# The last epilogue of a four-layer selective-scan network, run as four streams

## The chip, the cores and the metric

The kernel runs on one core of one Trainium2 chip. The metric is the device time of one execution in microseconds (us); smaller is better. The kernel before takes 21146.67 us, the median of three runs (21117.39, 21146.67 and 21153.36 us). One further execution was recorded by the hardware profiler; all profile numbers below are from that one.

A core has five engines, each with an instruction queue of its own: TensorE (PE) multiplies matrices and writes its sums to PSUM banks, VectorE (DVE) does elementwise work and scans, ScalarE (ACT) evaluates functions such as Exp, Ln and Silu, GpSimd (POOL) does elementwise work here, and SyncE (SP) issues the transfers (DMAs). An instruction waits at the head of its queue until the semaphores that it needs have been raised.

## The reference

The input is eight images of 48 by 48 positions and 96 channels. Four layers follow each other, each of the form x + ss2d(gn(x)), where gn normalises groups of three channels. Cut to what matters here, ss2d of a layer is:

```python
xz = x @ in_proj                       # 96 -> 2 * 192 channels
xc, z = split(xz)
xc = silu(depthwise_conv3x3(xc) + conv_b)
# four sequences: rows, columns, and both reversed
for each sequence: dt, B, C = projections of xc; delta = softplus(dt ...)
    h[t] = h[t-1] * exp(delta * A) + delta * u * B ; y[t] = sum_n h[t] * C
y = sum of the four sequences + D * xc
y = (y - mean(y)) * rsqrt(var(y) + eps) * g + b     # over the 192 channels
y = y * silu(z)
return y @ out_proj                    # 192 -> 96 channels
```

In the last layer the scan is written with cumulative sums (decay = exp(cumsum(...)), h = decay * cumsum(dB_u / (decay + 1e-12))). The last three lines of the block, together with z = x @ in_proj and the sum with x, are what this document calls the epilogue.

## The kernel before, in words

Two images form a pair, so each of the four layers has four pairs, and sixteen pairs are worked through one after the other. The 192 channels of two images are laid out as three tiles of 128 partitions. A pair has three parts. The **prologue** (`prologue`) normalises x, projects it, does the 3 by 3 convolution as nine products per block of rows (L301), and projects the scans' inputs. The **scans** are the main work: units that each handle some of the 16 states of one sequence. In the last layer only the first and last 192 positions of each sequence are scanned (class `Edge`): a pair has 48 units, twelve groups of four. The **epilogue** (`epilogue`) takes the sum y of the scans back from DRAM in 16 chunks of three image rows (144 positions) and finishes the layer.

`run` writes the program. Its loop goes over all units of all pairs. For each unit it writes the unit's own instructions: on ACT the logarithm and inverse of the decays (L887, L888) and four exponentials (L880); on PE the spreading of B (L893) and, four units late, the sum over states (L913); on DVE two products (L898, L899) and four scans (L901); on POOL two products (L905, L906). Beside it, it takes steps from two generators: the prologue of the following pair and the epilogue of the pair before. In the last layer up to ten such steps are written per unit. They begin at the fifth unit of a pair, and what is left of them is written in one go (`drain`) when the pair's last group of four units is reached. `prepare`, the softplus for the next group, is written in the first two units of each group (L585 to L614); it holds one of the two PSUM banks of the pool `psum` from its product L585 to L614.

After the last pair's scans nothing else is left to do beside it, and its epilogue is written by `drain(epilogue(*pairs[-1]))`: 16 chunks, one after the other. One chunk is this chain (line numbers of the kernel before):

1. PE: y minus its mean, as products with a centring matrix (L956, L957, L961, L962), into a PSUM bank.
2. ACT: copy to `eyc` (L996) and square into `ey` (L997); also the normalised x, `exn` (L990).
3. PE: minus the mean of the squares (L956 to L962 again).
4. ACT: Ln and Exp, together the inverse root (L1006, L1007).
5. DVE: product (L1009). ACT: gain and shift (L1012). PE: z (L1018, L1022).
6. ACT: Silu (L259), with a table load before it and another (L260) after it. DVE: product (L1031).
7. PE: x plus the output projection, twelve products (L1057, L1058, L1059). ACT: copy to `eo` (L1063). SP: two stores (L1065).

The loads of a chunk (`ex`, L972, and `ey`, L974) are issued in the middle of the chunk before it; both tiles have two buffers.

The generated order is not always the order of execution. The framework's scheduler sorts the instructions of each engine by its own model of costs. `keep_order(a, b)` takes this freedom away for a stretch of the program: it ties each instruction of an engine to the one written before it. The stretch is given by marks, that is by positions in the program that `mark()` appends to the list `marks`:

```python
        mark()                                  # once, before the first unit
...
            if l in short and unit == 0:
                mark()
...
    keep_order(*marks[:2])
```

`short` holds the last layer alone. In the kernel before, the stretch from the first unit to the first mark of the last layer keeps its written order; the last layer is left to the scheduler. A second program for the last layer behind a condition (`tc.If`) is not executed with these inputs.

Of the kernel before, what the change touches and what calls it, by code (L numbers as in the profile page):

```python
# [39 lines left out]
F32 = mybir.dt.float32  # L40
# [9 lines left out]
P = 128  # L50
NB, H, W, DM = 8, 48, 48, 96
# [18 lines left out]
BANK = 512  # L70
# [5 lines left out]
ECHUNKS = [(r * W, min(EROWS, H - r) * W) for r in range(0, H, EROWS)]  # L76
# [26 lines left out]
def ss2d_layers_kernel(ctx: ExitStack, tc: tile.TileContext, x_in, consts, weights, out):  # L103
# [14 lines left out]
    tmp = ctx.enter_context(tc.tile_pool(name="tmp", bufs=3))  # L118
# [131 lines left out]
    state = {}  # L250
# [11 lines left out]
    def bank():  # L262
        return psum.tile([P, BANK], F32, name="ps", tag="ps")
# [388 lines left out]
    class Chunk:  # L652
# [47 lines left out]
        def load(self, n):  # L700

            s, m, at = state[self.l, self.p], self.m, slice(self.c0, self.c0 + self.m)
            if n == 0:
                self.brow = rpool.tile([2 * NR, SCAN], BF16, name="brow", tag="brow")
                for j, b in enumerate(self.batches):
                    nc.sync.dma_start(
                        self.brow[NR * j : NR * j + NR, :m],
                        s["xb"][self.ph, b, :, self.d, :, at],
                    )
            row = 2 * layers[self.l].rank + 2 * NS * self.d + NS + n  # L710
            self.cb[n] = cb = cbpool.tile([P, SCAN], F32, name="cb", tag="cb")
            for b in self.batches:
                o = cb[64 * b : 64 * b + 64] if self.t == 2 else cb
                rows = s["xd"][self.ph, b, row : row + 1, at]
                nc.sync.dma_start(
                    o[:, :m], rows.to_broadcast([64 if self.t == 2 else P, m])
                )
# [221 lines left out]
                nc.sync.dma_start(s["yd"][t], y)  # L939


    def epilogue(l, p):
        ly, s = layers[l], state[l, p]
        gn, yd, src = s["gn"], s["yd"], x_store(l, p)
        dst = x_store(l + 1, p) if l + 1 < NLAYER else None
        EM = EROWS * W

        def half(b):
            return slice(64 * b, 64 * b + 64)

        def over_channels(ps, z, own, own_2, tiles):


            for t in tiles:
                if t < 2:
                    nc.tensor.matmul(ps[:, t, :], own, z[:, t, :], start=True, stop=False)  # L956
                    nc.tensor.matmul(ps[:, t, :], off_2[:, t, :], z[:, 2, :], start=False, stop=True)  # L957
                    continue
                for b in range(2):
                    o = ps[half(b), 2, :]  # L960
                    nc.tensor.matmul(o, off[:, 0:64], z[:, b, :], start=True, stop=False)  # L961
                    nc.tensor.matmul(o, own_2[:, half(b)], z[:, 2, :], start=False, stop=True)  # L962

        def three():
            return bank()[:, : 3 * EM].rearrange("p (t m) -> p t m", t=3)

        loaded = {}

        def load(i):
            at = slice(ECHUNKS[i][0], sum(ECHUNKS[i]))  # L970
            x = sm2.tile([DM, 2, EM], F32, name="ex", tag="ex")
            nc.sync.dma_start(x, src[:, :, at].rearrange("b c m -> c b m"))  # L972
            y = sm2.tile([P, 3, EM], F32, name="ey", tag="ey")
            nc.sync.dma_start(y, yd[:, :, at].rearrange("t p m -> p t m"))  # L974
            loaded[i] = x, y

        load(0)
        for _ in range(3):
            yield
        for i, (c0, m) in enumerate(ECHUNKS):  # L980
            at = slice(c0, c0 + m)
            x, y = loaded.pop(i)

            ps = three()
            over_channels(ps, y, centre, centre_22, (0, 1))
            yield True
            over_channels(ps, y, centre, centre_22, (2,))
            xn = sm1.tile([DM, 2, EM], F32, name="exn", tag="exn")
            for b in range(2):
                nc.scalar.activation(  # L990
                    xn[:, b, :], x[:, b, :], AF.Identity,
                    bias=gn[:, b, 1:2], scale=gn[:, b, 0:1],
                )
            yield True
            yc = sm1.tile([P, 3, EM], F32, name="eyc", tag="eyc")
            nc.scalar.copy(yc, ps)  # L996
            nc.scalar.activation(y, ps, AF.Square)  # L997
            yield

            ps = three()  # L1000
            over_channels(ps, y, off, off_22, (0, 1))
            yield True
            over_channels(ps, y, off, off_22, (2,))
            yield True

            nc.scalar.activation(ps, ps, AF.Ln, bias=ln_eps, scale=-1.0)  # L1006
            nc.scalar.activation(ps, ps, AF.Exp, scale=-0.5)  # L1007
            yield True
            nc.vector.tensor_mul(yc, yc, ps)  # L1009
            yield  # L1010
            for t, ts in ((0, slice(0, 2)), (2, slice(2, 3))):
                nc.scalar.activation(  # L1012
                    yc[:, ts, :], yc[:, ts, :], AF.Identity,
                    bias=ly.column(t, C_B), scale=ly.column(t, C_G),
                )
            ps = three()
            for t in range(2):
                nc.tensor.matmul(  # L1018
                    ps[:, t, :], ly.inw[:, DIN : DIN + P], xn[:, t, :], start=True, stop=True
                )  # L1020
            for b in range(2):
                nc.tensor.matmul(  # L1022
                    ps[half(b), 2, :], ly.inw[:, DIN + P : 2 * DIN], xn[:, b, :],
                    start=True, stop=True,
                )
            if i + 1 < len(ECHUNKS):
                load(i + 1)
            yield True
            silu(ps, ps)
            yield True  # L1030
            nc.vector.tensor_mul(yc, yc, ps)  # L1031
            yield
            if dst is not None:
                ps = bank()[0:DM, : 2 * EM].rearrange("p (b m) -> p b m", b=2)
                for b in range(2):
                    nc.tensor.matmul(
                        ps[:, b, :], ident[0:DM, 0:DM], x[:, b, :], start=True, stop=False
                    )
                    nc.tensor.matmul(
                        ps[:, b, :], ly.outw[:, 0, :], yc[:, b, :], start=False, stop=False  # L1040
                    )
                    nc.tensor.matmul(
                        ps[:, b, :], ly.outw_2[:, b, :], yc[:, 2, :], start=False, stop=True
                    )
                yield True
                nc.scalar.copy(x, ps)
                yield
                nc.sync.dma_start(dst[:, :, at].rearrange("b c m -> c b m"), x)
                continue

            q = m // 2
            ps = bank()[:q, : 4 * DM].rearrange("q (h b c) -> q h b c", h=2, b=2)
            for h in range(2):
                z = slice(h * q, h * q + q)
                for b in range(2):
                    o = ps[:, h, b, :]
                    nc.tensor.matmul(o, x[:, b, z], ident[0:DM, 0:DM], start=True, stop=False)  # L1057
                    nc.tensor.matmul(o, yc[:, b, z], ly.outw[:, 0, :], start=False, stop=False)  # L1058
                    nc.tensor.matmul(o, yc[:, 2, z], ly.outw_2[:, b, :], start=False, stop=True)  # L1059
            yield True  # L1060
            st = sm2.tile([P, 4, DM], F32, name="eo", tag="ld")
            st = st[:q].rearrange("q (h b) c -> q h b c", h=2)
            nc.scalar.copy(st, ps)  # L1063
            for b in range(2):
                nc.sync.dma_start(  # L1065
                    out[2 * p + b, at, :].rearrange("(h q) c -> q h c", h=2), st[:, :, b, :]
                )
            yield
        del state[l, p]


    def drain(g):
        for _ in g:
            pass
# [22 lines left out]
    def mark():  # L1097
        marks.append(len(tc._region_blocks()[0].instructions))

    def keep_order(a, b):  # L1100

        last = {}
        info = mybir.DependencyInfo(mybir.DependencyClass.NoSync, mybir.DependencyReason.DATA)
        for i in tc._region_blocks()[0].instructions[a:b]:
            if i.engine in ENGINES:
                if i.engine in last:
                    tc.add_manual_dep(i, last[i.engine], info, reason="order")
                last[i.engine] = i.name
# [5 lines left out]
    def run(pairs, short):  # L1114
# [102 lines left out]
            c.add_up(n)  # L1217
            catch_up()
        collected()
        drain(epilogue(*pairs[-1]))  # L1220

    last = NLAYER - 1
    run([(l, p) for l in range(NLAYER) for p in range(NPAIR)], (last,))

    keep_order(*marks[:2])


    every = sm1.tile([P, 1], F32, name="every", tag="every")
# [102 lines left out]
```

## Time and profile before

| what | us |
|---|---|
| median of three runs | 21146.67 |
| the profiled execution | 21131.57 |
| its span, first to last instruction | 21129.7 |
| last layer, pair 0 (first L880 of the pair to that of the next) | 19223.6 to 19650.4 |
| pair 1 | 19650.4 to 20087.8 |
| pair 2 | 20087.8 to 20522.8 |
| pair 3, to its last sum (L935) | 20522.8 to 20893.0 |
| last epilogue, first product to end of the last copy | 20900.2 to 21122.9 |

| engine | busy us in the span | share |
|---|---|---|
| PE | 18566.6 | 88% |
| DVE | 18834.4 | 89% |
| ACT | 13520.6 | 64% |
| POOL | 17984.5 | 85% |

The profile is read by stretches here, because the shares of the whole span are those of the three long layers. In a line of the table of stretches, the numbers are the start and end, the length, then for PE, PEld (TensorE's loading of weights), DVE, ACT and POOL the busy time and, in brackets, the number of instructions; then the clock that was granted to TensorE as a share of the full one, the share of DMA time, and GB/s. In the chain, each line is a start, a duration, and the engine and line that the end of the program hung on at that moment.

### The profile page before, as it was taken

Reading aid. Unit: us, or ns where it says so; the run is one execution under the profiler, and the core shown is the slowest. Engines: PE = TensorE matmul, PEld = TensorE weight load, DVE = VectorE, ACT = ScalarE, POOL = GpSimd, SP = SyncE. Lnnn points to the kernel's source line nnn. Section 1 sums busy time; section 2 is a strip of 40 time slices with the busy share of each in tenths; the row PEclk is TensorE's granted clock in tenths of the full one; section 3 lists DMA queues with packets and bytes.
Section 4 is the critical chain, followed back from the end, with each engine's and each line's share of the span. In section 5 each row is a group of like instructions: output and inputs, shape, how many; then the busy total and the mean of one; then the engine's idle time right before and its main releaser. Section 6 shows DMA issues by size and latency. Waiting matters only on the chain. (4 is left out here: it accounts for less than half of the span.)

```text
span 21129.7 us, 229163 instructions
## 1 busy us (share of the span) xinstructions
PE 18566.6 (88%) x64610; PEld 9118.1 (43%) x64610; DVE 18834.4 (89%) x15938; ACT 13520.6 (64%) x23969; POOL 17984.5 (85%) x11081
## 2 busy tenths in 40 slices
PE   8988998998998998998998988998998998988886
PEld 3333444443444443443443443443443443444555
DVE  6999999999999999999999999999999999997453
ACT  5555666666666665665666666665665666667776
POOL 5999898898899899898899989898999899896442
PEclk8999999999999999999999999999999999999887
DMA  4666666676676676676676666666666666674221
GB/s 137 195 193 193 188 196 194 190 196 195 190 200 195 192 201 195 190 204 191 191 204 195 191 194 195 190 197 190 191 197 193 190 196 195 189 194 123 79 74 51
DMA packets 1707632, 3832.96 MB, mean 181 GB/s; under 512 B 238448, under 2 KB 575216, under 8 KB 1693168
## 3 DMA queue, kind: packets, MB, share of 16 engines
q1 hardware_dynamic: 1706352, 3818.21, 61.9%
q8 instruction: 521, 8.54, 0.2%
q14 instruction: 759, 6.22, 0.1%
HBM read 3665.08 MB, written 152.27 MB: 181 GB/s over the span
## 5 line engine op out<-in xcount | busy, mean ns | idle before, releaser
L804 PE MATMUL acc<-cb,cst 128*128 128x384 f32 x27648 | 10706.0, 516 | 0.0
L768 POOL TENSOR_TENSOR cb<-cb,da 128x768 f32<-128x768 f32 x5184 | 9349.5, 1813 | 1393.2 <-DVE da L759 875.6
L804 PEld LDWEIGHTS acc<-cb,cst 128*128 128x128 f32 x27648 | 5003.6, 196 | 3957.4 <-issue 1498.2
L759 DVE TENSOR_TENSOR_SCAN da<-da,carry,b 128x768 f32<-128x768 f32 x3456 | 6268.3, 1814 | 220.9 <-ACT b L726 3.7
L755 DVE TENSOR_TENSOR b<-du,b 128x768 f32<-128x768 f32 x5184 | 4912.0, 948 | 685.4 <-PE b L743 678.8
L726 ACT ACTIVATE da<-dl,a 128x768 f32<-128x768 f32 x5184 | 4770.4, 926 | 95.6 <-POOL cb L768 60.4
L743 PE MATMUL b<-brow,pick 48*128 48x512 bf16 (+3 forms) x10368 | 2652.0, 337 | 1581.8 <-DVE da L759 1239.4
L726 ACT ACTIVATE b<-dl,a 128x768 f32<-128x768 f32 x1728 | 1560.3, 903 | 2960.1 <-DVE da L759 2817.4
L698 POOL TENSOR_TENSOR bb<-bb,du 128x768 f32<-128x768 f32 x1728 | 3131.3, 1812 | 183.4 <-DMA bb<-xd 142.8
L768 POOL TENSOR_TENSOR cb<-cb,bb 128x768 f32<-128x768 f32 x1728 | 3134.0, 1814 | 161.5 <-issue 56.8
L759 DVE TENSOR_TENSOR_SCAN da<-da,b 128x768 f32<-128x768 f32 x1728 | 3030.5, 1754 | 110.2 <-ACT b L726 2.4
L743 PEld LDWEIGHTS <-pick 48*128 48x128 bf16 (+1 forms) x10368 | 669.2, 97 | 4379.9 <-DVE da L759 2363.1
L759 DVE TENSOR_TENSOR_SCAN bb<-b,carry,bb 128x768 f32<-128x768 f32 x1152 | 2069.3, 1796 | 5.9 <-ACT b L726 2.2
L301 PE MATMUL ps<-pad,diag 128*128 128x480 f32 (+1 forms) x4320 | 2015.0, 565 | 15.1 <-DVE du L611 9.6
L650 ACT COPY carry<-da 128x1 f32<-128x1 f32 x3456 | 627.1, 181 | 1086.3 <-DVE da L759 1076.4
L590 ACT ACTIVATE ps<-ps,w 128x384 f32<-128x384 f32 (+1 forms) x912 | 497.1, 545 | 1027.5 <-PE ps L585 1022.9
L301 PEld LDWEIGHTS ps<-pad,diag 128*128 128x128 f32 x4320 | 804.2, 193 | 725.2 <-issue 330.3
L603 POOL TENSOR_TENSOR lg<-lg,w 128x384 f32<-128x384 f32 (+1 forms) x912 | 892.4, 978 | 195.0 <-ACT w L601 194.8
L585 PE MATMUL ps<-dts,w 6*128 6x384 f32 (+5 forms) x2432 | 821.2, 523 | 240.6 <-DVE du L611 99.9
L759 DVE TENSOR_TENSOR_SCAN bb<-b,bb 128x768 f32<-128x768 f32 x576 | 1000.1, 1736 | 16.3 <-POOL bb L698 9.8
L604 POOL TENSOR_TENSOR lg<-lg,e 128x384 f32<-128x384 f32 (+1 forms) x912 | 889.5, 975 | 71.2
L798 PE MATMUL acc<-y,cst 128*128 128x384 f32 x1008 | 619.1, 745 | 192.2 <-ACT y L819 127.2
(141 smaller groups left out, 17243.9 us busy)
## 6 DMA issues: line engine op xcount, KB each, us to landing
cb<-xd SPq DMA_DIRECT2D x4736, 384.0 KB
cb<-xd SPq DMA_DIRECT2D x4736, 192.0 KB
bb<-xd SPq DMA_DIRECT2D x1152, 384.0 KB
bb<-xd SPq DMA_DIRECT2D x1152, 192.0 KB
yd<-y SPq DMA_DIRECT2D x48, 1152.0 KB
ey<-yd SPq DMA_DIRECT2D x256, 216.0 KB
brow<-xb SPq DMA_DIRECT2D x576, 72.0 KB
ex<-xs SPq DMA_DIRECT2D x256, 108.0 KB
```

The source lines that it names most:

```text
L301: nc.tensor.matmul(ps[:, :m], ly.diag[:, int(t == 2), j, :], pad[:, r0 + dy : r0 + dy + nr, dx : dx + W], start=(j == 0), stop=(j == 8),)
L585: nc.tensor.matmul(o[:, :m], ly.dtw[q0 : q0 + r, k, chans], dts[q0 : q0 + r, at], start=True, stop=True,)
L603: nc.gpsimd.tensor_sub(lg, lg, w1)
L604: nc.gpsimd.tensor_add(lg, lg, e)
L650: nc.scalar.copy(*late_act.pop(0))
L698: nc.gpsimd.tensor_mul(b, b, self.du)
L726: nc.scalar.activation(da, self.dl, AF.Exp, scale=columns_of(self.l, self.t, self.ph, self.d, n))
L743: nc.tensor.matmul(b[:, z : z + zm], w, self.brow[:k, z : z + zm], start=True, stop=True)
L755: nc.vector.tensor_mul(b, self.du, b)
L759: nc.vector.tensor_tensor_scan(way(h), way(da), way(b), start, ALU.mult, ALU.add)
L768: nc.gpsimd.tensor_mul(c, c, h)
L804: nc.tensor.matmul(self.acc[:, a, : self.m // 2], ident, c[:, a, :], start=False, stop=(n == NS - 1 and not self.turns),)
```

## The change

The epilogue of the last pair becomes four generators. Stream 0 takes chunks 0, 4, 8 and 12, stream 1 takes 1, 5, 9 and 13, and so on. `run` steps through them in turns; stream i is left out until turn 3 * i, so each begins three steps behind the one ahead of it. A chunk has twelve steps. Streams 0 and 1 take their PSUM tiles from `psum`, streams 2 and 3 from `pb`, the pool of the scans' B (two buffers each). Streams 1 to 3 hold x, the normalised x, y and its centred form in one tile `ew` of the pool `tmp` (three buffers, otherwise used by prologues) and load a chunk when they begin it; stream 0 loads ahead as before. Two marks are set around the streams, and a second `keep_order` is added.

```diff
+        def own_bank():
+            return bank() if part < 2 else pb.tile([P, 2 * BANK], F32, name="b", tag="b")
...
         def load(i):
             at = slice(ECHUNKS[i][0], sum(ECHUNKS[i]))
-            x = sm2.tile([DM, 2, EM], F32, name="ex", tag="ex")
+            if part:
+                w = tmp.tile([P, 10 * EM], F32, name="ew", tag="tmp")
...
+            else:
+                x = sm2.tile([DM, 2, EM], F32, name="ex", tag="ex")
+                y = sm2.tile([P, 3, EM], F32, name="ey", tag="ey")
+                xn = yc = None
...
-        load(0)
+        mine_of = range(part, len(ECHUNKS), parts)
+        load(part)
         for _ in range(3):
             yield
-        for i, (c0, m) in enumerate(ECHUNKS):
+        for i in mine_of:
+            c0, m = ECHUNKS[i]
             at = slice(c0, c0 + m)
-            x, y = loaded.pop(i)
+            if i not in loaded:
+                load(i)
+            x, y, xn, yc = loaded.pop(i)
...
-            if i + 1 < len(ECHUNKS):
-                load(i + 1)
+            if not part and i + parts < len(ECHUNKS):
+                load(i + parts)
...
-        drain(epilogue(*pairs[-1]))
+        mark()
+        streams = [epilogue(*pairs[-1], part, 4) for part in range(4)]
+        turn = 0
+        while streams:
+
+            streams = [g for i, g in enumerate(streams) if turn < 9 and turn < 3 * i or next(g, g) is not g]
+            turn += 1
+        mark()
...
     keep_order(*marks[:2])
+    keep_order(*marks[2:4])
```

The instructions of the epilogue and their shapes are the same; the lines of the changed kernel are numbered 1 to 22 higher from L957 on (L956 is L957, L996 is L1018, L1006 is L1028, L1012 is L1034, L1031 is L1053, L1057 is L1079, L1063 is L1085, L1065 is L1087).

More of the change, by code (lines that the diff above doesn't have):

```diff
@@ L939, in collect, with epilogue @@
                 nc.sync.dma_start(s["yd"][t], y)
-    def epilogue(l, p):
+    def epilogue(l, p, part=0, parts=1):
         ly, s = layers[l], state[l, p]
@@ L962, in over_channels @@
                     nc.tensor.matmul(o, own_2[:, half(b)], z[:, 2, :], start=False, stop=True)
+        def own_bank():
+            return bank() if part < 2 else pb.tile([P, 2 * BANK], F32, name="b", tag="b")
         def three():
-            return bank()[:, : 3 * EM].rearrange("p (t m) -> p t m", t=3)
+            return own_bank()[:, : 3 * EM].rearrange("p (t m) -> p t m", t=3)
         loaded = {}
@@ L970, in load @@
             at = slice(ECHUNKS[i][0], sum(ECHUNKS[i]))
-            x = sm2.tile([DM, 2, EM], F32, name="ex", tag="ex")
+            if part:
+                w = tmp.tile([P, 10 * EM], F32, name="ew", tag="tmp")
+                x, xn = (
+                    w[:DM, a * EM : a * EM + 2 * EM].rearrange("p (b m) -> p b m", b=2)
+                    for a in (0, 2)
+                )
+                y, yc = (
+                    w[:, a * EM : a * EM + 3 * EM].rearrange("p (t m) -> p t m", t=3)
+                    for a in (4, 7)
+                )
+            else:
+                x = sm2.tile([DM, 2, EM], F32, name="ex", tag="ex")
+                y = sm2.tile([P, 3, EM], F32, name="ey", tag="ey")
+                xn = yc = None
             nc.sync.dma_start(x, src[:, :, at].rearrange("b c m -> c b m"))
-            y = sm2.tile([P, 3, EM], F32, name="ey", tag="ey")
             nc.sync.dma_start(y, yd[:, :, at].rearrange("t p m -> p t m"))
-            loaded[i] = x, y
-        load(0)
+            loaded[i] = x, y, xn, yc
+        mine_of = range(part, len(ECHUNKS), parts)
+        load(part)
         for _ in range(3):
             yield
-        for i, (c0, m) in enumerate(ECHUNKS):
+        for i in mine_of:
+            c0, m = ECHUNKS[i]
             at = slice(c0, c0 + m)
-            x, y = loaded.pop(i)
+            if i not in loaded:
+                load(i)
+            x, y, xn, yc = loaded.pop(i)
             ps = three()
@@ L987, in epilogue @@
             over_channels(ps, y, centre, centre_22, (2,))
-            xn = sm1.tile([DM, 2, EM], F32, name="exn", tag="exn")
+            if xn is None:
+                xn = sm1.tile([DM, 2, EM], F32, name="exn", tag="exn")
             for b in range(2):
@@ L994, in epilogue @@
             yield True
-            yc = sm1.tile([P, 3, EM], F32, name="eyc", tag="eyc")
+            if yc is None:
+                yc = sm1.tile([P, 3, EM], F32, name="eyc", tag="eyc")
             nc.scalar.copy(yc, ps)
@@ L1051, in epilogue @@
             q = m // 2
-            ps = bank()[:q, : 4 * DM].rearrange("q (h b c) -> q h b c", h=2, b=2)
+            ps = own_bank()[:q, : 4 * DM].rearrange("q (h b c) -> q h b c", h=2, b=2)
             for h in range(2):
@@ L1068, in epilogue @@
             yield
-        del state[l, p]
+        state[l, p]["left"] = state[l, p].get("left", parts) - 1
+        if not state[l, p]["left"]:
+            del state[l, p]
     def drain(g):
```

## The prediction

> **What bounds the kernel now.** I read the page first, for the place of the stretch in the span.
>
> ```profile
> span 21129.7 us, 229163 instructions
> ...
> PE   8988998998998998998998988998998998988886
> ...
> POOL 5999898898899899898899989898999899896442
> PEclk8999999999999999999999999999999999999887
> ```
>
> Each digit is 528 us. Only the last is about the stretch that the change names: TensorE at 0.6, POOL at 0.2, and a granted clock of 0.7. So the next view is the table of stretches: the last layer's pairs 0 to 3, then what follows its last sum.
>
> ```profile
> 19223.00:19650.00 427.00, 355.95 (x1804) 239.15 (x1803) 228.80 (x403) 340.94 (x635) 194.07 (x136) 0.91 0.31 87
> 19650.00:20088.00 438.00, 368.87 (x1982) 255.25 (x1982) 225.11 (x394) 344.33 (x643) 191.98 (x135) 0.88 0.27 75
> 20088.00:20522.00 434.00, 366.74 (x1982) 253.20 (x1982) 219.86 (x382) 342.63 (x640) 189.81 (x130) 0.89 0.27 73
> 20522.00:20893.00 371.00, 251.16 (x1618) 207.08 (x1617) 214.05 (x375) 287.07 (x545) 181.25 (x116) 0.81 0.24 67
> 20893.00:21130.00 237.00, 153.65 (x1026) 130.80 (x1026) 19.52 (x34) 118.26 (x190) 0.00 (x0) 0.73 0.14 35
> ```
>
> In the last row no engine is full: TensorE 65%, ACT 50%. The chain (one chunk, its longer pieces) says why: one engine works at a time.
>
> ```profile
> 20926.98 0.59 PE ps L1058 x2
> ...
> 20930.78 0.53 PE ps L956 x2
> ...
> 20933.38 0.52 ACT eyc L996
> ...
> 20936.40 0.60 ACT ps L1006
> ...
> 20937.56 1.28 ACT L259
> ...
> 20940.33 0.61 DVE eyc L1031
> ...
> 20940.98 0.59 PE ps L1058 x2
> ```
>
> The chunk's period is 14.0 us here, 13.7 on average (L996 at 20919.38 and, fourteen chunks later, 21110.96). From the first product at 20900.2 to the end of the last copy at 21122.9, the sixteen take 222.7.
>
> **What the order says.** The title speaks of instructions taken in their order. `keep_order(*marks[2:4])` doesn't do that to the epilogue. `mark()` is called once before the first unit and at unit 0 of every pair of the last layer, four times, before the two new calls: marks 2 and 3 are the starts of pairs 1 and 2. The listing of each engine's order in the changed program agrees. In pair 1 the places where an engine steps back against the written order go from 65 (PE), 71 (DVE), 130 (ACT), 46 (POOL) and 60 (SP) to none. In the epilogue 13 remain on PE and 26 on ACT: the scheduler still sorts it. So the change has two parts: four streams, and pair 1 (row two above) pinned to its written order. Pair 0 keeps its order within; pairs 2 and 3 change in a few per cent of places, taken as nothing.
>
> **What the Trainium skill says.** "TensorE: Matmul & The Clock Gate", What's actually happening: TensorE falls to half rate after an idle window of about 3.4 us and returns after as much sustained work. The trace agrees in kind: after 2.4 us idle before L1058 at 20926.98, pairs of L956 and L957 products follow each other in 0.48 us; from 20934.9 on in 0.24. "Perfetto Trace Analysis", Tensor Engine Instruction: ACT, DVE and GpSimd are strict FIFO, and PE only pulls weight loads ahead. No line here contradicts it; an order that is pinned is thus the order of waiting. "ScalarE: Activation LUTs", What ACT_TABLE_LOAD costs: 1283 ns plus a drain of 1380. The trace shows 1.28 and the next function 0.02 later, so 1.28 is used. "DMA: Bandwidth & Descriptors", Anatomy of one DMA: semaphores are waited for by the issuing engine. So a load waiting for its tile holds SP's later transfers.
>
> **Part one, the streams.** No product, function or byte is added; the listing has 32 table loads in both (16 chunks, two each). Work of a chunk: ACT 7.45 us (stretch 20927 to 20941), DVE 1.2, TensorE 9.7 at the present mixed clock. At full clock: second mean 1.9 (20934.39 to 20936.32), so the first also 1.9, z 1.2 (20922.21 to 20923.37), output 2.0 (half of 20926.98 to 20930.78): 7.0. Streams three steps apart put four chunks' steps into every three turns: turn a has 2.0 of TensorE and two DVE products, turn b 5.0 of TensorE and 1.9 of ACT, turn c 5.6 of ACT. Following the queues through four such groups by hand, TensorE comes round after 33 us, 8.3 a chunk; the longest hole is 3.6 us, where the square of one stream stands behind another's Silu with its two tables.
>
> Added: streams 1 to 3 have one tile each, so a load can leave only after the chunk's last product. Landing took 2.8 us (20897.25 to 20900.03), issue 0.3 for each of two; the next product is due 2 to 4.6 us after, so about 1 us is uncovered: 9.3 a chunk. Behind such a load in SP's queue stand other streams' stores, and for those only `eo`, two chunks later, waits. PSUM: `pb` is idle after the scans, and `tmp` has no prologue: no wait.
>
> Turns: 48 for a stream and 9 for the offsets, 57. The middle 39 are 13 chunks' worth, 121 us; the 18 with one to three streams lie between 13.7/4 = 3.4 and 9.3 per three, 6.4 taken: 38; start and end 4. Sum 163 against 223: **60 saved**. Bounds: ACT alone, 16 x 7.45 plus 10 of filling, saves 93; TensorE staying at 9.7 with 1.5 of holes, plus 10, 189, saves 33.
>
> **Part two, pair 1 in written order.** Before, in three stretches:
>
> ```profile
> 19650.00:19671.00 21.00, 12.82 (x57) 10.13 (x57) 17.16 (x30) 15.92 (x34) 17.47 (x12) 0.66 0.19 60
> 19671.00:20042.00 371.00, 331.55 (x1781) 226.48 (x1781) 195.82 (x344) 299.16 (x555) 165.33 (x112) 0.92 0.27 74
> 20042.00:20088.00 46.00, 24.51 (x146) 18.64 (x146) 12.12 (x24) 29.25 (x55) 9.18 (x12) 0.69 0.29 86
> ```
>
> TensorE is 89% busy in the middle, because the scheduler slid side work into the holes. Written order:
>
> - Units 1 to 4, no side work: 21 us as before.
> - Units 5 to 43: TensorE's work is 369 less what stands before and after, 13 and about 38, so 318. Holes: I followed nine units (9 to 17) by hand, with ACT 3.3 (L887, L888, four L880), TensorE 2.2 (L893, L913) per unit, 0.8 per convolution product (109.8 us for 270 halves), 2.1 per mean. TensorE works 80 us and needs 97. The holes: after z, 3.4 us per chunk (L1012 1.0, table 1.28, Silu 0.52, L1031 0.6), with the output next in its queue; between the means, 0.8, as the copy stands behind ACT's 3.3 of the next unit; and 3 to 4 us per group while `prepare` holds one of two banks and ACT, in L609, waits for POOL and DVE. That is 1.9 a unit, 74; some ten units in which ACT has more than TensorE (9.8 against 7.5) add 2 each. 318 + 74 + 18 = 410.
> - Unit 44: about 3.7 chunks drained with nothing between, 13.7 each, 51, and the rest of the projections 4: 55. DVE and POOL stand still behind it.
> - Units 45 to 48: 18.
>
> Sum 504 against 438: **66 lost**, and about 1 at the border with pair 0, whose last sums overlapped more with pair 1 (96 TensorE products after pair 1's first, now 37). Bounds: no hole at all leaves 369 and a start of about 40, a gain of 30; if every hole also costs a slow clock for its next 3 us, 1.5 a chunk and group more, and ACT's waits add up, 110 lost.
>
> **Sum.** -60 + 66 + 1 = +7 us on the profiled 21131.57, 21139. The median stands 15 above the profiled execution, so 21146.67 + 7, about **21154**.
>
> **Rivals.**
> *Pinning costs nothing* (0.17): the streams gain 60 and pair 1 loses less than 15. For it: the three long layers run pinned at 0.9 and more of TensorE. Against it: they write at most one side step per unit, not ten. Net -50 to -80: about 21085.
> *Pinning costs most* (0.31), the other side: pair 1 loses 110 through the serial waits in ACT's queue, or the streams gain 35 because TensorE stays at half rate; from a loss 42 above the gain on it decides. For it: the clock row of the last stretch, 0.73; the 46 us tail at 0.69. Net +45 to +90: about 21210.
> *The streams don't overlap*, as loads wait in SP's queue behind each other: 16 chunks at 12, gain 25, net +40. Against: DMA is at 0.14 there. It lies at the border of the likeliest and the slow case and is counted in these.
>
> **Chances.** 0.2% (42 us) is about what a measurement can tell from no change. Likeliest, the halves cancel to within 42 either way: 0.52, its own range 21112 to 21185. Faster 0.17, slower 0.31. For eight in ten I leave out the lower part of the first rival and the upper part of the second: 21088 to 21225.
>
> **What would show it.** Right: the stretch from the last L935 to the end falls from 237 to 170 to 185 us, its clock rises above 0.85, and squares wait behind table loads; pair 1, first L880 to that of pair 2, grows from 437 to about 500, with a stretch of some 50 us without POOL before its last four units, then four units at the end; pairs 0, 2 and 3 stay within 5 us. Wrong: pair 1 below 455 (the written order has no such holes), or above 545; an epilogue above 190 (loads, or the clock). The number would also fail if the scheduler's small moves in pairs 2 and 3 cost more than 5 us each.

## The result and the profile after

The changed kernel takes 21181.51 us (median of 17 runs, 21152.10 to 21226.63); beside it the kernel before took 21150.37 (17 runs, 21112.88 to 21171.08). The ratio is 1.0018, with a 95% interval of 1.0010 to 1.0025: slower by 31 us between the medians, 37 between the means. The interval leaves out 1, but the difference is under the 0.2% that the prediction called no change. The forecast was 21154, in a range of 21088 to 21225.

The page of the changed kernel, its first lines; a digit of the rows is 529 us:

```profile
span 21179.7 us, 229015 instructions
...
PE   8988988998998998988998988988988988988787
...
POOL 5999898999899899899899989899898899896343
PEclk9999999999999999999999999999999999999888
```

The last digit of TensorE rises from 6 to 7 and its clock from 0.7 to 0.8; in the third digit from the end (19591 to 20121 us) TensorE falls from 8 to 7 and POOL from 4 to 3. Something was won at the very end and given back some time before. The table of stretches of the changed kernel says where: start and end, length, then busy time and instructions of PE, PEld, DVE, ACT and POOL, the granted clock, the DMA share and GB/s. The first four rows are the four parts of pair 1 that the prediction told apart, then pairs 2 and 3, what follows the last sum, and a stretch from the middle of that.

```profile
19649.00:19672.00 23.00, 11.39 (x48) 9.05 (x47) 17.11 (x30) 16.48 (x36) 15.52 (x10) 0.66 0.25 84
19672.00:20137.00 465.00, 351.44 (x1632) 231.10 (x1633) 184.65 (x315) 281.58 (x513) 151.59 (x105) 0.82 0.20 56
20137.00:20204.00 67.00, 40.34 (x252) 32.79 (x250) 15.39 (x27) 32.63 (x56) 6.45 (x10) 0.74 0.21 51
20204.00:20231.00 27.00, 13.39 (x42) 10.15 (x42) 12.60 (x21) 16.97 (x37) 17.39 (x13) 0.50 0.22 63
20231.00:20671.00 440.00, 373.49 (x2018) 261.02 (x2019) 223.50 (x395) 347.84 (x647) 193.98 (x133) 0.90 0.29 81
20671.00:21045.00 374.00, 255.55 (x1618) 210.53 (x1617) 213.30 (x374) 288.01 (x548) 181.00 (x116) 0.80 0.24 67
21045.00:21180.00 135.00, 108.37 (x1026) 94.91 (x1026) 19.39 (x34) 110.14 (x184) 0.00 (x0) 0.95 0.22 59
21080.00:21140.00 60.00, 55.14 (x543) 48.69 (x543) 10.27 (x17) 59.49 (x102) 0.00 (x0) 1.00 0.24 60
```

The last stretch shrank from 237 to 135 us, and in its middle ACT works 59.49 of 60 us; TensorE comes second with 55.14. The same 1026 products of TensorE take 108.37 us there instead of 153.65. Pair 1 went the other way. Its long middle part is 465 us instead of the 410 foreseen, and TensorE idles in 114 of them. Both parts left the marks that the prediction had set: its sign of a wrong sum was a pair 1 above 545 us, and the last stretch is below its 170 to 185.

To compare runs, all pairs are counted alike from here on, from the first exponential (L880) written for a pair to that of the next. That is a few units earlier than in the table of the kernel before; the length of its pair 1 is 437.4 us by either count. Profiled executions, us:

| kernel | pair 0 | pair 1 | pair 2 | pair 3 | after the last sum | profiled execution |
|---|---|---|---|---|---|---|
| before | 432.6 | 437.4 | 435.7 | 377.3 | 236.7 | 21131.57 |
| after | 429.2 | 578.1 | 445.0 | 380.9 | 134.7 | 21181.58 |
| difference | -3.4 | +140.7 | +9.3 | +3.6 | -102.0 | +50.0 |

The five differences sum to +48. The medians differ by 31 only because the profiled execution of before lies 19 us below its median of 17 runs, while that of after lies at its own. The lengths of stretches repeat well: six profiles in which pair 1 is left free have it at 434.9 to 437.6, two in which it is pinned on all engines and nothing else is changed there at 578.1 and 579.4, and seven in which the four streams are left to the scheduler, with the same work on ACT, take 134.3 to 136.8 after the last sum.

### The profile page after: what moved, and what is told of

It reads as the page before. It is cut to its first block, busy times and chain, and to the rows that moved or that the text cites. A ratio compares the mean times of both kernels' runs of the same rounds, so it can differ in the third digit from the quotient of the medians.

```text
span 21179.7 us, 229015 instructions
## 1 busy us (share of the span) xinstructions
PE 18588.0 (88%) x64610; PEld 9117.8 (43%) x64610; DVE 18835.2 (89%) x15938; ACT 13520.4 (64%) x23965; POOL 17992.1 (85%) x11081
## 5 line engine op out<-in xcount | busy, mean ns | idle before, releaser
L301 PE MATMUL ps<-pad,diag 128*128 128x480 f32 (+1 forms) x4320 | 2025.7, 567 | 20.6 <-DVE du L611 9.6
L301 PEld LDWEIGHTS ps<-pad,diag 128*128 128x128 f32 x4320 | 806.8, 194 | 732.5 <-issue 332.3
L585 PE MATMUL ps<-dts,w 6*128 6x384 f32 (+5 forms) x2432 | 821.8, 523 | 259.5 <-DVE du L611 90.3
L759 DVE TENSOR_TENSOR_SCAN bb<-b,bb 128x768 f32<-128x768 f32 x576 | 1000.0, 1736 | 14.2 <-ACT b L726 7.1
L607 DVE SCALAR_TENSOR_TENSOR ps<-ps,lg 128x384 f32<-128x384 f32 (+1 forms) x912 | 485.4, 532 | 343.1 <-POOL lg L604 342.8
```

What stands on the lines that cost most here:

```text
L301: nc.tensor.matmul(ps[:, :m], ly.diag[:, int(t == 2), j, :], pad[:, r0 + dy : r0 + dy + nr, dx : dx + W], start=(j == 0), stop=(j == 8),)
L585: nc.tensor.matmul(o[:, :m], ly.dtw[q0 : q0 + r, k, chans], dts[q0 : q0 + r, at], start=True, stop=True,)
L759: nc.vector.tensor_tensor_scan(way(h), way(da), way(b), start, ALU.mult, ALU.add)
```

## The experiments

The theory at the start was the prediction's: two independent parts, streams that gain and a pinned pair 1 that loses. Every kernel here does the whole computation.

### One part without the other

The streams alone, pair 1 left to the scheduler:

```diff
 keep_order(*marks[:2])
-keep_order(*marks[2:4])
```

> The four streams without the second keep_order. Theory (two independent parts): the stretch after the last L935 stays at 135 us as in the changed kernel (before: 237), pair 1 goes back to 437 us, so about 100 us under the kernel before, a ratio of 0.9953. Rival (the streams gain only in company of the pinned pair, or the scheduler's other choices in pairs 2 and 3 cost): less than 60 us under.

The kernel before with pair 1 pinned and nothing else:

```diff
 keep_order(*marks[:2])
+keep_order(*marks[2:4])
```

> The kernel before with keep_order(*marks[2:4]) alone. Theory: pair 1 grows from 437 to 582 us as in the changed kernel, pairs 0, 2 and 3 change by less than 6 us, the epilogue stays at 237; about 145 us over the kernel before, a ratio of 1.0069. Rival (part of pair 1's growth comes from the streams, by buffers or the scheduler): under 110 us over.

| kernel | pair 1 | after the last sum | median, us | ratio to before (95%) |
|---|---|---|---|---|
| streams alone | 437.6 | 136.4 | 21049.20 | 0.9954 (0.9937 to 0.9970) |
| pin alone | 579.4 | 236.6 | 21280.35 | 1.0070 (1.0053 to 1.0087) |

The kernel before took 21137.50 beside these two and the next one (median of 38 runs). Each part does in its own place what it does in the whole change, and nothing in the other's. The two effects on the time, -0.46% and +0.70%, add up to +0.24%, and the whole gives +0.18% with an interval up to +0.25%. So the split is settled, and both sizes are larger than foreseen.

### The order that the title speaks of

The marks of the epilogue are 5 and 6. Here the tie is put there, and pair 1 is free:

```diff
-keep_order(*marks[2:4])
+keep_order(*marks[5:7])
```

> The streams with the second keep_order on the streams' own marks, marks[5:7], and pair 1 left to the scheduler. Theory: ACT was busy 110 of the 112 us in which the streams ran, so the written order can't gain; it loses what the scheduler's 26 moves on ACT saved: 0 to 15 us above the streams alone, 85 to 100 under the kernel before. Rival (the written order is the better one): 10 us or more below the streams alone.

Measured: 21100.32 us, ratio 0.9980 (0.9973 to 0.9987), and 201.8 us after the last sum against 136.4 with the scheduler's order. That is a miss by several times what was expected: the written order is 65 us slower in the profiled stretch and 51 us in the medians. Its middle in the table of stretches (same columns as above):

```profile
20922.00:21080.00 158.00, 113.96 (x872) 102.12 (x872) 17.18 (x29) 101.61 (x169) 0.00 (x0) 0.81 0.13 33
```

ACT works 64% of it and TensorE 72%, at a clock of 0.81. The waits of this kernel in the stretch (engine, line, what it waited for, us in total, times, longest), those of PE, and of ACT on a load:

```profile
PE b L957 <- ACT ew L1019: 20.5, 8, 4.2
PE b L957 <- DMA ew<-yd: 17.2, 6, 3.2
...
ACT ew L1011 <- DMA ew<-xs: 6.1, 3, 2.1
...
PE ps L957 <- DMA ew<-yd: 3.9, 2, 2.0
```

and two entries of its timeline (start, length, engine, line, operands, and in brackets the idle time before and who ended it):

```profile
20977.35 0.91 ACT L1011 ACTIVATE ew<-ew,gn 96x144 f32<-96x144 f32 x2 [2.02 <-DMA ew<-xs]
20978.48 0.82 PE L957 MATMUL b<-ew,centre 128*128 128x144 f32 x2 [3.12 <-DMA ew<-yd]
```

In written order a stream's square (L1019) stands in ACT's queue behind another stream's work, TensorE stands at the head of its own queue with the product that needs it, and nothing may pass. Likewise a late reload holds up everything behind its first user. With the scheduler's order the same waits are these (streams alone, same columns):

```profile
PE ps L957 <- ACT ew L1019: 2.8, 4, 1.0
PE b L957 <- ACT ew L1019: 1.9, 6, 0.4
PE b L957 <- DMA ew<-yd: 1.3, 3, 0.5
```

Which queue's order matters was asked next. `keep_order` got a list of engines:

```diff
-def keep_order(a, b):
+def keep_order(a, b, engines=ENGINES):
...
-        if i.engine in ENGINES:
+        if i.engine in engines:
```

The epilogue kept on all engines but SP, `engines=[e for e in ENGINES if e != mybir.EngineType.SP]`:

> The streams in written order on PE, DVE, ACT and POOL, SP left to the scheduler; pair 1 not pinned. With all five kept, what follows the last sum takes 202 us, with none 136. Theory A (the reloads of the single tiles, 27 us of waits for ew in the kept run, are what the scheduler hides by issuing them earlier): 160 to 180. Theory B (the order on TensorE and ACT, which meet the load too early): 190 or more.

and on TensorE alone, `engines=[mybir.EngineType.PE]`:

> The streams in written order on TensorE alone. Theory A: 145 or less, since SP and ACT are free. Theory B (TensorE comes to a stream's first product before its reload can have landed, and everything behind waits): 165 or more.

| epilogue kept on | after the last sum | TensorE clock | one run, us |
|---|---|---|---|
| nothing (streams alone) | 136.4 | 0.94 | 21062.52 (profiled) |
| TensorE | 168.5 | 0.87 | 21069.36 |
| all but SP | 176.9 | 0.83 | 21099.45 |
| all | 201.8 | 0.78 | 21107.88 (profiled) |

With SP free the stretch lies in the range of the first theory, that of the reloads; with TensorE alone kept it lies in that of the second, but the waits for squares are longer than those for reloads, which that theory had named. TensorE's order alone makes 32 of the 65 us: its products on the banks of the scans wait 19.9 us for squares (L1019), eight times, as in the fully kept order, but 8.9 us for reloads (`ew`) instead of 21.1. SP's order makes the last 25: with SP free and the rest kept, the wait for reloads is 8.6 us. ACT, DVE and POOL together add 8 between the two. These are differences along one path of adding engines; another path may share them out differently. Only the stretch is compared here, since single times of one kernel scatter by tens of us (the changed kernel's 17 by 75).

### What pinning costs in pair 1

The first waits that the prediction had not foreseen were on loads, so SP was let free in pair 1:

```diff
-keep_order(*marks[2:4])
+keep_order(*marks[2:4], engines=[e for e in ENGINES if e != mybir.EngineType.SP])
```

> The changed kernel with pair 1 pinned on TensorE, DVE, ACT and POOL, and SP's transfers left to the scheduler. Theory A (the loads written just before their use are what the prediction left out): pair 1 falls from 582 to 540 to 555 us, and L585 waits for no DMA. Theory B (the order of the computing engines and the slow clock are all of it): pair 1 stays above 570.

Then TensorE alone pinned, and ACT alone (`[mybir.EngineType.PE]`, `[mybir.EngineType.Activation]`):

> The changed kernel with pair 1 pinned on TensorE alone. With all five engines pinned pair 1 takes 578 us, without SP 557, with none 437. Theory A (TensorE's queue is what the written order spoils: the output stands before the convolution products while z waits for Silu, and the scheduler had moved those): 530 us or more. Theory B (ACT's queue: the main logarithms and exponentials stand behind side functions that wait for TensorE): under 490.

> The changed kernel with pair 1 pinned on ACT alone. Theory A (TensorE's queue): pair 1 under 490 us. Theory B (ACT's queue): 530 or more. If both this and TensorE alone give over 530, the order written in the program forces itself through either queue, as each instruction of the one waits for the other's.

Pair 1 of the kernels in this order: before, TensorE pinned, ACT pinned, all but SP, all. One answer of the table of stretches from each profile:

```profile
19643.00:20080.00 437.00, 368.44 (x1982) 255.19 (x1982) 224.14 (x393) 343.35 (x641) 191.42 (x134) 0.88 0.27 75
```

```profile
19641.00:20136.00 495.00, 391.19 (x1958) 269.78 (x1957) 221.11 (x385) 346.33 (x642) 188.20 (x133) 0.83 0.22 64
```

```profile
19667.00:20174.00 507.00, 393.70 (x1960) 265.61 (x1961) 224.16 (x389) 346.88 (x644) 188.40 (x134) 0.82 0.21 59
```

```profile
19640.00:20197.00 557.00, 403.12 (x1948) 275.36 (x1947) 223.20 (x382) 347.54 (x644) 183.91 (x135) 0.82 0.21 58
```

```profile
19641.00:20219.00 578.00, 409.44 (x1948) 277.32 (x1947) 222.59 (x382) 346.62 (x640) 183.94 (x135) 0.79 0.20 56
```

Letting SP free gives back 21 us of the profiled pair, a little less than expected, and L585 waits for no transfer there. The median is 21156.11, ratio to before 1.0011 (1.0004 to 1.0018); this interval and that of the changed kernel overlap, so the whole times alone don't resolve it. The other two ran once each: 21094.21 with TensorE pinned, 21138.54 with ACT pinned. TensorE's order alone costs 58 and ACT's alone 69; with DVE and POOL they cost 119 together. No single queue is the cause, and neither pair of expectations was met: each theory had one of the two queues carry most of the loss. Busy times of ACT, DVE and POOL stay within 8 us in all five rows. TensorE's rises from 368 to 409 with slightly fewer products in the stretch, while its clock falls from 0.88 to 0.79, and its idle time rises from 69 to 169. So of +141 us, 41 are the same products taking longer and 100 are new idle time. This split is read from busy times; no run forced the clock while leaving the holes.

What TensorE, and the engines it feeds, wait for in the middle part of the changed kernel (waits, same columns as before):

```profile
ACT u L309 <- PE ps L301: 65.7, 15, 8.2
...
PE ps L1080 <- DVE eyc L1053: 18.4, 4, 9.6
PE ps L585 <- DMA dts<-xd: 18.1, 5, 6.1
...
PE ps L369 <- DVE mv L366: 12.6, 2, 6.6
...
PE ps L957 <- ACT ey L1019: 9.1, 5, 2.8
...
PE ps L301 <- DVE eyc L1031: 6.0, 4, 2.0
```

The first row is ACT standing at a copy of the convolution's rows, 65.7 us; over the whole pair of the kernel before it stands there 14.0. Four others, the rows of L1080, L369, L957 and L301, are holes of the kind that the prediction followed by hand: a product at the head of the queue, and its operand some steps away on ACT and DVE. The third row is another kind: the weight product of a group (L585) waits for `dts`, whose load is written directly ahead of it, in the same step of `prepare`. Over the whole pair it waits 30.3 us, 12.2 of them in the last four units, and not at all in the kernel before. Was that load simply too late? Here it is written two units earlier:

```diff
-if n == 10 and coming_to + 1 < len(chunks):
+if n == (2 if l in short and p == 1 else 10) and coming_to + 1 < len(chunks):
```

> The changed kernel with all of pair 1 pinned, and its dts loads written one group of units earlier (at the third unit of a group, not inside prepare). If the waits of L585 for dts, 18 us in the trace of the changed kernel, are most of SP's 21 us, pair 1 falls from 578 to 556 to 563 us. If they only hide other waits, it stays above 572.

Measured: the 18.1 us of the middle are gone; the 12.4 at the end remain; that load is for pair 2's first group, which the edit doesn't reach. Pair 1 is 568.2 us, 10 shorter (one run, 21150.37), and lies between the two expectations. So nearly half of the wait taken away had covered other waits: a line of waits is not a sum that can be handed back.

Nor is the end of the pair the cure. With 13 side steps a unit instead of 10 less should be left to drain after unit 44:

```diff
-for _ in range(10 if l in short else 0 if ends else 1):
+for _ in range(13 if l in short and p == 1 else 10 if l in short else 0 if ends else 1):
```

> The changed kernel, all of pair 1 pinned, with thirteen side steps written per unit in pair 1 instead of ten, so that hardly anything is left for the drain before its last four units. If that drain (67 us in the changed kernel, with POOL and DVE nearly idle) is a cost of its own, pair 1 falls from 578 us by 20 to 40. If the holes belong to the side steps wherever they are written, it stays within 10 us.

Pair 1 took 618.9 us, 41 more (one run, 21234.61): a miss for every expectation, though the drain did go: the longest break between POOL's products L905 and L906 around the pair's end, 62.9 us in the changed kernel, is no longer there (the longest in the pair is 27.2). With more side steps between a unit's own instructions in a fixed order, each of these stands behind more; ACT's wait at the convolution's rows (L309) grew from 65.7 us to 90.4. That reading was not tested further.

### A version that beats both

ACT is the fullest engine of the streams, and DVE works 19 of 135 us there. Gain and shift (L1034) and the normalised x (L1011) go to DVE, with nothing pinned:

```diff
-keep_order(*marks[2:4])
...
 for b in range(2):
+    if parts > 1:
+        nc.vector.tensor_scalar(
+            xn[:, b, :], x[:, b, :], gn[:, b, 0:1], gn[:, b, 1:2], ALU.mult, ALU.add
+        )
+        continue
     nc.scalar.activation(
...
 for t, ts in ((0, slice(0, 2)), (2, slice(2, 3))):
+    if parts > 1:
+        nc.vector.tensor_scalar(
+            yc[:, ts, :], yc[:, ts, :], ly.column(t, C_G), ly.column(t, C_B),
+            ALU.mult, ALU.add,
+        )
+        continue
     nc.scalar.activation(
```

> The streams alone, pair 1 not pinned, with the normalised x (L1011) and the gain and shift (L1034) of the four streams on DVE instead of ACT. ACT is 99% busy there, 7.0 us a chunk; 1.9 of it goes. If ACT is the bound and TensorE, 6.8 us a chunk, comes next, the 136 us after the last sum fall to 120 to 132, 4 to 16 us under the streams alone, so 105 to 115 under the kernel before. If TensorE is as tight as ACT, no change within 4 us.

Its last stretch, from the table of stretches:

```profile
20887.00:21017.00 130.00, 107.03 (x1026) 94.91 (x1026) 36.44 (x90) 86.88 (x128) 0.00 (x0) 0.94 0.23 61
```

ACT is relieved of 23 us and DVE takes 17 more; TensorE, at 107 of 130, is now the fullest engine, so the stretch shrinks by 7 only. The median is 21023.31 us, ratio 0.9946 (0.9932 to 0.9959), against 0.9954 for the streams alone: faster than the kernel before and the changed one, by about half a per cent. Whether it beats the streams alone is not resolved by the times, only by the profiled stretch (129.6 against 134.3 to 136.8 in seven profiles of the streams with ACT's work left on ACT).

## Why the prediction was right, and where it was not

The time fell into the forecast's own range of the likeliest case (21112 to 21185), 3.5 us below its upper end. Both terms were too small: 60 gained became 102, and 66 lost became 141. The mechanism, two opposite parts that nearly cancel, was right and is shown by the two separate runs. The sizes were not. Each broke its own bound, and the time was hit because errors of 42 and 75 us have opposite signs: that is luck.

- **"The scheduler still sorts it", and the marks.** Right. Where the tie does lie on the epilogue, the stretch differs by 65 us, so the question of which pair the marks enclose was worth more than most durations in the sum.
- **Streams, 60 saved (33 to 93).** Too small, and the upper bound broke. Two steps failed. First, the rotation was followed in its written order, with a hole of 3.6 us and 1 us of uncovered reload per chunk, although the text had just said that this order isn't executed. In the executed order both are nearly gone (ACT idles 0.5 us of the middle 60, reloads cost 1.5 us in all). As a picture of the kept order the steps were right in kind (squares behind other streams' work, late reloads) and 25 us too cheap: 163 us worked out, and 14 before the first product and after the last copy (237 less 222.7), make 177, and the kept run needs 202. So the 9.3 us a chunk were the term that failed: in the middle 60 us nine chunks pass (L259 loads nine tables), 6.7 each. Second, the bound "ACT alone, 16 x 7.45", 119.2 us, took a chunk's ACT time from a stretch in which its instructions mostly waited for each other; measured are 110.14. Kept fed, they overlap more: the instructions of the changed kernel's last stretch last 121.7 us in sum, 11.6 more than ACT's busy time, where in the kernel before it was 124.3 in 118.26, 6.0 more. The other part is work that ran ahead: eight of the 32 L1011 (4 us) lie before the stretch, the first of them at 20661. The Trainium skill has this overlap ("ScalarE: Activation LUTs", What ACT_TABLE_LOAD costs: about 93 ns between neighbouring ACTIVATEs), and the bound held only as much of it as the waiting chain showed.
- **"Its clock rises above 0.85".** Right: 0.95, and 1.00 in the middle. The 153.65 us of TensorE became 108.37, 6.8 a chunk where the prediction had 7.0 at full clock; so 45 us of what looked like work before was slowness. The Trainium skill's "TensorE: Matmul & The Clock Gate", What's actually happening, which ties the rate to how busy TensorE has been, fits both ends of the change: 0.73 to 0.95 in the epilogue, 0.88 to 0.79 in pair 1. The clock records of these traces know only the full rate and half of it, and change in steps of 3.41 us. But the idle window of about 3.4 us, in which the prediction saw an agreement "in kind", is not what they show. From 20905 to 21120 us, in the last epilogue of the kernel before, TensorE is never idle for more than 2.4 us, and yet its rate falls to half 16 times. Each fall follows a step in which TensorE was busy 36% to 65% of the time, each return one in which it was busy throughout. There, holes well short of 3.4 us were enough to cost the full rate.
- **"Squares wait behind table loads".** Wrong for the changed kernel: TensorE waits for squares 4.6 us in its epilogue (17.0 in that of the kernel before). It is true of the kept order, for 20.5 us on two of the streams: from 20985 to 20990 us there, for example, ACT runs another stream's Silu with both its tables ahead of the square, and TensorE idles 2.5 us.
- **Pair 1, 504 us (bounds -30 to +110).** Too small: 578 (582 by the four rows above). The 66 us were all idle time, as TensorE's busy time was left at the 369 of the kernel before; idle time rose by 100, and busy time by 41. (The ten units with 2 us each were entered as 18, not 20; that changes nothing.) The step that failed first is "318" for TensorE's work in units 5 to 43: it measured 351, at a clock of 0.82, where the durations came from a stretch at 0.92. The slow clock stood in the upper bound alone, though the step had counted holes, and the 46 us at the end of the pair, with holes in them, stood in the table at 0.69. The second is the holes, 92 foreseen and 114 measured: the count held no wait for a transfer, though SP was one of the pinned queues. SP's order is worth 21 (the run without it); the load of `dts`, written earlier, gave back 10.
- **Unit 44's drain, 55, measured 67.** Its chunks took 56.7 us and not 51 (20137 to 20193.67; the last three stand 14.2 apart, L1018 at 20153.17, 20167.57 and 20181.61). The rest of the projections was put at 4; it took 10.3 of this stretch and went on in the next, as a string of transfers through DRAM. From the chain of the changed kernel (start, length, what):

```profile
20181.61 0.52 ACT eyc L1018
...
20193.67 2.98 PE ps L454 x8
20196.67 0.47 ACT xe L509
20197.17 4.50 DMA xd<-xe
20202.10 1.71 DMA raw<-xd
...
20208.72 2.98 DMA dts<-xd
```

  From the end of the last chunk at 20193.67 to the last landing at 20211.7 are 18 us, of which products are 3. In the kernel before, the chain of that place holds the 4.43 us of `xd` from `xe` too, but TensorE waits for no `dts` there. The last four units took 27 and not 18: TensorE waits 12.2 for `dts`, whose load stands in SP's queue behind the stores of L445 (20202.56; the load leaves at 20208.72). That this load is the cause is not shown: with SP free, the product L585 that waited comes early, and TensorE waits 12.2 us all the same, before a later L585 and for DVE's L611.
- **Pairs 2 and 3 as nothing.** Roughly right, though pair 2 left the 5 us that the prediction had allowed: +9 and +4 in the profiled execution, +5 and +4 with the pin alone, +4 and +6 with the streams alone. No cause was sought.
- **The rivals.** "Pinning costs nothing" fell: the three long layers' pinned order says little about a pair with ten side steps a unit. "Pinning costs most" named the size of pair 1 better than the likeliest case did (110, measured 141), though ACT's order alone costs 69, half of that. It didn't decide the time, by little: it needed a loss 42 us above the gain, and 141 - 102 is 39. "The streams don't overlap" fell, with 135 us.

What stays open: how clock and holes share the loss of pair 1 when one is changed without the other, why more side steps a unit cost 41 us more, and the small growth of pairs 2 and 3.

## What to carry to other kernels

Before costing an order, establish by position which instructions a tie encloses, and take the executed order, not the written one, for everything outside it. A written order that interleaves many dependent chains is an order of waiting: here it cost 65 us in an epilogue of 136 and 141 in a pair of 437, on TensorE's, ACT's and SP's queues alike, so free it or pin only stretches with slack. When holes are added ahead of TensorE, add to their length the slower products that follow, even if each hole is short, and look at DMAs that the old order had hidden.

## What was not expected of the hardware

Back to back, ACT's instructions start closer together than they are long. From the timeline of the changed kernel in the middle of the streams (start, length, engine, line):

```profile
21095.65 0.52 ACT L1018 COPY ew<-b 128x432 f32<-128x432 f32 x1
21096.06 0.53 ACT L1029 ACTIVATE ps<-ps 128x432 f32<-128x432 f32 x1
21096.51 0.53 ACT L1019 ACTIVATE ew<-b 128x432 f32<-128x432 f32 x1
21096.93 0.47 ACT L1085 COPY eo<-b 72x384 f32<-72x384 f32 x1
```

Neighbours that need nothing of each other follow after 0.41 to 0.45 us, though each lasts 0.52: an overlap of 0.08 to 0.11, close to what the page named above has. One that needs its neighbour's result doesn't: in the last epilogue of the kernel before, the Exp (L1007) starts 0.03 us after the end of the Ln (L1006) that it reads, all 16 times. So durations added up overstate what an engine needs when it is kept full: here 121.7 us took 110.14, a tenth less, and in the chain of the kernel before, with more waiting, 124.3 took 118.26, a twentieth less. The difference was enough to help break a bound that was meant to be firm.
